# Attention b: the row maxima moved into the query tiles by one transpose, one copy and two small transfers

## The chip, the cores and the metric

The kernel runs on one core of a Trainium2 chip. The metric is the device time of one execution in microseconds (us). The core has five engines, each of which takes its own instructions in order: PE (TensorE, matrix multiplies and transposes; its weight loads are shown as PEld), DVE (VectorE), ACT (ScalarE), POOL (GpSimd) and SP (SyncE, which here only starts DMA transfers). Engines wait for each other by semaphores.

## What is computed

Four layers are added to a residual x of 2 x 512 x 512 numbers: attention a, a mixture of experts, attention b, and the same mixture of experts again. The change is in attention b, cut here to what matters (B = 2, T = 512, 32 query heads, 8 key heads, 16 numbers each):

```python
x = x + _L0_attn_b_ref(_layernorm(x, axis=-1), Wq, Wk, Wv, Wo)
...
att = jnp.einsum('bhgqd,bhkd->bhgqk', qg, k) / math.sqrt(D_HEAD)
att = jnp.where(causal[None, None, None], att, -jnp.inf)
probs = jax.nn.softmax(att, axis=-1)
ctx = jnp.einsum('bhgqk,bhkd->bhgqd', probs, v)
```

The softmax needs the largest score of every query. The kernel finds it in a first pass over the scores and subtracts it in a second one.

## The kernel before

Attention a comes first (to about 720 us in the trace). Then comes a short stretch of experts and projections, and then the stage of attention b, which this change is in: it begins with the first score at 792.6 us and the last product of the second pass begins at 1025 us. What follows is the end of attention b for the second batch entry and the last experts.

**Pairs and steps.** The heads of attention b are worked on in 32 pairs (`pairs`). A pair takes 3 steps (`STEPS`), and there are 104 steps. PE's order is written out by hand (`manual_schedule` for PE); the order on the other engines is made by the framework's scheduler. A step emits, in this order: now and then the loading of query rows (`queries_halved`, `queries_in`); in one step of three, `maxima_in` for a pair; a third of `probabilities` for a pair; a third of `maxima` for a later pair; sometimes four calls of `weighted_b`; and a piece of side work (projections of the second batch entry, later the output projection and the experts).

**First pass**, `maxima` (lines 765 to 797), pair p in steps 3p to 3p+2. PE multiplies queries by keys into PSUM tiles `sc` (line 781), and DVE adds the causal mask and takes the maxima into a small tile `top` (line 785): a query on each of 128 partitions, 4 query tiles, 2 heads. After the last part POOL splits each maximum into a rounded part and a rest (lines 793 and 794). They go into a tile `mm` of 4 x 66 columns, of which only columns 0, 1 and 64, 65 are ever filled; two such tiles exist, and both are set to zero once (line 609).

**Into rows**, `maxima_in` (lines 799 to 807), in step 3p+4. The second pass needs the maxima in rows 64 and 65 of the query tile `qs`, one row for the rounded parts and one for the rests, 2 heads x 512 queries each. The keys hold -1 in those rows, so that the product of keys and queries comes out with the maximum subtracted. PE transposes the four 66-column parts of `mm` into one PSUM tile `tpm` (line 804), and ACT copies two rows of it for each head into `qs` (line 807).

**Second pass**, `probabilities` (lines 812 to 845), pair p in steps 3p+8 to 3p+10 (`LEAD` is 8). PE multiplies keys by queries, the maximum included, into PSUM tiles `st` (line 828); ACT takes the exponential (line 834); POOL clears the part above the diagonal (line 837). `weighted_b` then multiplies by the values on PE (line 854). It runs for two pairs together.

**Shared buffers.** `sc`, `st` and `tpm` use one ring of five PSUM banks (`ps_x`), in the order in which they are emitted. A tile waits until the one five places before it has been read: `sc` by DVE, `st` and `tpm` by ACT. There are five query tiles `qs`. Pair p uses the tile of pair p-5, and its load (line 761, on SP) and the clearing of its rows 64 and 65 by POOL (line 763, needed because the first pass must not see old maxima) are emitted in step 3p-4. Both wait for the last `st` of pair p-5.

The lines which place these calls in a step are:

```python
            if at == 0 and 2 <= p < len(pairs):
                queries_in(p)
            p, at = divmod(step - 4, STEPS)
            if at == 0 and 0 <= p < len(pairs):
                maxima_in(p)
            if LEAD <= step:
                next(ps)
            if step < total:
                next(ms)
```

Of the kernel before, what the change touches and what calls it, by code (L numbers as in the profile page):

```python
# [11 lines left out]
F32 = mybir.dt.float32  # L12
I32 = mybir.dt.int32
F32R = mybir.dt.float32r
AF = mybir.ActivationFunctionType
ALU = mybir.AluOpType
# [3 lines left out]
P = 128  # L20
B, S, DM = 2, 512, 512
NT = S // P
# [18 lines left out]
def kernel(  # L41
# [21 lines left out]
    nc = tc.nc  # L63
# [3 lines left out]
    small = ctx.enter_context(tc.tile_pool(name="small", bufs=4))  # L67


    x = {}  # L70
# [7 lines left out]
    ident = const.tile([P, P], F32, tag="ident", name="ident")  # L78
# [201 lines left out]
    with ExitStack() as actx:  # L280
# [226 lines left out]
        def chain(*stages):  # L507
            for stage in stages:
                yield from stage
# [13 lines left out]
        for n in range(len(units) + 4):  # L523
            turn = []

            def at(lag):
                if 0 <= n - lag < len(units):
                    g, b, h = units[n - lag]
                    return (g, b, h, f"{g}_{b}_{h}")

            if at(3):
                g, b, h, nm = at(3)
# [4 lines left out]
            if at(0):  # L537
                g, b, h, nm = at(0)
# [8 lines left out]
            if at(4):  # L547
                g, b, h, nm = at(4)
                turn.append(output(wo[g], h, g * A_G + h, b, *ats.pop((g, b, h)), nm))
            if at(2):  # L550
                g, b, h, nm = at(2)
# [22 lines left out]
    w2 = ctx.enter_context(tc.tile_pool(name="w2", bufs=1))  # L574
# [11 lines left out]
    for sp in range(4):  # L586
        for par in range(2):
            at = sp * STRIP + par * B_HD
# [9 lines left out]
    HALF, HM = P // 2, P // 2 + 2  # L598
    NQ = 5
    qs = [w2.tile([P, 2, S], F32, tag=f"qs{n}", name=f"qs_{n}") for n in range(NQ)]  # L600
    ks = [w2.tile([P, 4, S], F32, tag=f"ks{n}", name=f"ks_{n}") for n in range(2)]

    mmp = [w2.tile([P, NT, HM], F32R, tag=f"mm{n}", name=f"mm_{n}") for n in range(2)]

    vpads = [
        w2.tile([P, NT, 2, 4, STRIP], F32, tag=f"vpad{n}", name=f"vpad_{n}") for n in range(B)
    ]
    for pad in (*ks, *qs, *vpads, *(mm.bitcast(F32) for mm in mmp)):
        nc.gpsimd.memset(pad, 0.0)
    for pad in ks:  # L610
        nc.gpsimd.memset(pad[HALF:HM], -1.0)
# [10 lines left out]
    dram = ctx.enter_context(tc.tile_pool(name="dram", bufs=2, space=bass.MemoryType.DRAM))  # L622
# [99 lines left out]
    STEPS, LEAD = 3, 8  # L722
    mms, nums, oNs, pTs = {}, {}, {}, {}
# [6 lines left out]
    def spread(hl, nm, order):  # L730
# [5 lines left out]
            )  # L736
        return to.rearrange("n (d h) s -> (n d) h s", h=B_NKV)

    kparts, qparts = {}, {}

    def keys_in(b, kh):

        if kh == 0:
            kparts[b] = spread(khls[b], f"k_{b}", (slice(0, 4, 2), slice(1, 4, 2)))
        nc.sync.dma_start(ks[kh][:HALF], kparts[b][:, ts(kh, 4), :])

    def queries_halved(p):

        b, kh, g, _ = pairs[p]
        hl = hlp.tile([P, 2, S], F32R, tag="hl", name=f"hl_{p}")  # L750
        src = qTs[b][:, kh * 2 + g // 2, :]
        nc.scalar.copy(hl[:, 0, :], src)
        nc.gpsimd.tensor_tensor(hl[:, 1, :], src, hl[:, 0, :].bitcast(F32), ALU.subtract)
        to = spread(hl, f"q_{p}", (slice(0, 2), slice(2, 4)))
        for n in range(4):
            qparts[p + n] = to

    def queries_in(p):
        _, _, g, pr = pairs[p]
        q = qs[p % NQ]  # L760
        nc.sync.dma_start(q[:HALF], qparts.pop(p)[:, ts((g % 2) * 2 + pr, 2), :])
        if p >= NQ:
            nc.gpsimd.memset(q[HALF:HM], 0.0)

    def maxima():

        for p, (b, kh, g, pr) in enumerate(pairs):
            q, k = qs[p % NQ].bitcast(F32R), ks[kh].bitcast(F32R)
            top = small.tile([P, NT, 2], F32, tag="top", name=f"top_{p}")
            for tiles in ((0, 1), (3,), (2,)):  # L770
                sc = [
                    ps_x.tile([P, S], F32, tag="x", name=f"sc_b_{p}_{tiles[0]}_{h}")
                    for h in range(2)
                ]
                parts, at = [], 0
                for i in tiles:
                    n = (i + 1) * P
                    parts += [(i, n, h, sc[h][:, at : at + n]) for h in range(2)]
                    at += n
                for i, n, h, part in parts:  # L780
                    nc.tensor.matmul(  # L781
                        part, q[:, h, ts(i, P)], k[:, pr * 2 + h, :n], start=True, stop=True
                    )
                for i, n, h, part in parts:
                    nc.vector.tensor_tensor_reduce(  # L785
                        part, part, tri[:, S - n :], 1.0, -3e38, ALU.add, ALU.max,
                        top[:, i, h : h + 1],
                    )
                if tiles == (2,):
                    mm = mms[p] = mmp[p % len(mmp)]  # L790
                    for h in range(2):
                        at = (1 - h) * HALF
                        nc.gpsimd.tensor_copy(mm[:, :, at], top[:, :, h])
                        nc.gpsimd.tensor_tensor(
                            mm[:, :, at + 1], top[:, :, h], mm[:, :, at].bitcast(F32), ALU.subtract
                        )
                yield

    def maxima_in(p):

        mm = mms.pop(p).bitcast(F32)
        tp = ps_x.tile([P, S], F32, tag="x", name=f"tpm_{p}")
        for t in range(NT):
            nc.tensor.transpose(tp[:HM, ts(t, P)], mm[:, t, :], ident)
        for h in range(2):
            at = (1 - h) * HALF
            nc.scalar.copy(qs[p % NQ][HALF:HM, h, :].bitcast(F32R), tp[at : at + 2, :])


    due = []  # L810
# [92 lines left out]
    def output_b(b, cs):  # L903

        while not all((b, c) in ready for c in cs):
            yield MM
        for i in range(NT):
            po = place("bank", [P, DM], f"po_{b}_{i}_{cs[0]}")
            for c in cs:
                nc.tensor.matmul(  # L910
                    po, oNs[b, c][:, ts(i, P)], wo2[:, c, :], start=(c == cs[0]), stop=(c == cs[-1])
                )
                if c == cs[-1]:
                    nc.vector.tensor_tensor(x[b, i], x[b, i], po, ALU.add)
                yield MM

    def run(*stages):
        stages = list(stages)
        while stages:
            stages = [st for st in stages if next(st, stages) is not stages]  # L920
# [18 lines left out]
    for p in range(2):  # L939
        queries_in(p)  # L940
    parts(later, 14)

    ms, ps = maxima(), probabilities()
    total = len(pairs) * STEPS
    half = total // 2
# [3 lines left out]
    for step in range(total + LEAD):  # L949
        with tc.manual_schedule(engines={mybir.EngineType.PE}):  # L950
            if step == LEAD:
                pace = 0.95
            if step == half - 4:
                run(side)
                keys_in(1, 0)
                queries_halved(len(pairs) // 2)
                side = output_b(0, (0, 1))
                pace, left = 0.37, 0.0
            if step == half + LEAD:
                keys_in(1, 1)  # L960
            if step == half + LEAD + 10:
                side = chain(side, output_b(0, (2, 3)), experts(0, "f2", True))
                pace, left = 0.95, 0.0
            if step == total - 6:
                side = chain(output_b(1, (0, 1)), side)
                pace, left = 1.4, 0.0
            quotients[:] = [q for q in quotients if next(q, None) is not None]
            p, at = divmod(step + 4, STEPS)
            if at == 0 and p % 4 == 3 and p + 1 < len(pairs) and p + 1 != len(pairs) // 2:
                queries_halved(p + 1)  # L970
            if at == 0 and 2 <= p < len(pairs):
                queries_in(p)
            p, at = divmod(step - 4, STEPS)
            if at == 0 and 0 <= p < len(pairs):
                maxima_in(p)
            if LEAD <= step:
# [4 lines that stand above are left out]
            if len(due) > 3 and due[3][0] <= step:  # L981
                for _ in range(4):
                    weighted_b(*due.pop(0)[1])
            left += pace
            while left > 0:
                got = next(side, None)
                if got is None:
                    left = 0.0
                else:
                    left -= got  # L990
# [99 lines left out]
```

## Time and profile before

| what | value |
|---|---|
| median of 3 runs | 1092.24 us (1091.74 to 1095.13) |
| the profiled execution's own time | 1095.07 us |
| its span, first to last instruction | 1093.4 us |
| PE busy | 1046.9 us, 96% of the span |
| DVE busy | 859.0 us, 79% |
| ACT busy | 627.2 us, 57% |
| POOL busy | 598.5 us, 55% |
| TensorE clock granted, mean | 0.992 of full speed |

The profiled execution is one of its own and lies 2.8 us above the median of the runs; 1.7 us of its time are outside the span. A busy share is an average over the whole span. What a change is worth must be read from the stage that it is in. In rows of the profile, a time in ns is the mean of one instruction, and what stands after the second bar is how long the engine was idle just before, with the instruction whose end it waited for. DMA-issuing instructions are not counted as busy.

### The profile page before, as it was taken

How to read it: one execution, taken by the hardware profiler on the slowest of the kernel's cores; microseconds unless marked ns; L12 is line 12 of the kernel's file. 1: busy time of each engine (PE TensorE's matmuls, PEld its weight loads, DVE VectorE, ACT ScalarE, POOL GpSimd, SP SyncE). 2: the span in 40 equal slices, each digit the busy share in tenths (PEclk: the TensorE clock that was granted, in tenths of full speed). 3: DMA queues.
4: the chain of work that ended last, by engine and by line, in shares of the span. 5: the costliest groups of instructions: out<-in, count | busy, mean ns of one | idle time of the engine just before them, and what ended most of it. 6: DMA issues, size and time to landing. Idle time of an engine off the chain costs nothing.

```text
span 1093.4 us, 16248 instructions
## 1 busy us (share of the span) xinstructions
PE 1046.9 (96%) x4940; PEld 707.0 (65%) x4940; DVE 859.0 (79%) x2175; ACT 627.2 (57%) x1475; POOL 598.5 (55%) x916
## 2 busy tenths in 40 slices
PE   5799999999999999999999999999999999999988
PEld 3477767777777677777777777556467655565534
DVE  6889899999999999999999999574386667766142
ACT  3666666567666566566666665513166567685410
POOL 2466666677576666666666666262245566554200
PEclk9999999999999999999999999999999999999999
DMA  7301011012110010010021000042342235211011
GB/s 294 116 1 39 1 39 39 1 39 78 39 40 25 16 39 20 20 39 12 28 75 42 1 1 1 1 155 75 87 161 83 57 122 149 88 49 35 28 38 39
DMA packets 23271, 60.47 MB, mean 55 GB/s; under 512 B 4369, under 2 KB 5329, under 8 KB 20369
## 3 DMA queue, kind: packets, MB, share of 16 engines
q1 hardware_dynamic: 23184, 59.44, 16.4%
q8 instruction: 40, 0.66, 0.2%
q14 instruction: 47, 0.38, 0.1%
HBM read 45.53 MB, written 12.85 MB: 53 GB/s over the span
## 4 chain that ended last, share of the span: by engine, by line
PE 80%; DVE 9%; ACT 4%; issue 2%; POOL 2%; DMA 2%; SPq 0%; ACTq 0%; POOLq 0%; DVEq 0%
PE sc L412 11%; PE av L445 11%; PE tp L440 6%; PE ph_f L207 5%; PE ps_q L365 5%; PE ps_o L457 5%; PE ps_o L458 5%; PE ps_q L366 4%; PE st_b L828 4%; PE py_f L266 3%; PE sc_b L781 3%; PE num_b L854 3%; PE po L910 3%; PE pq_b L701 2%; DVE r_q L372 1%
## 5 line engine op out<-in xcount | busy, mean ns | idle before, releaser
L429 POOL TENSOR_SCALAR p<-p,rden 128x128 f32<-128x128 f32 (+3 forms) x256 | 152.4, 607 | 227.0 <-DVE rden L427 167.1
L420 ACT ACTIVATE p<-sc,nmx 128x128 f32<-128x128 f32 (+3 forms) x256 | 135.8, 530 | 110.3 <-DVE nmx L415 108.7
L412 PE MATMUL sc<-kT,qT 128*128 128x128 f32 (+3 forms) x512 | 180.5, 435 | 1.7 <-ACT p L420 1.3
L372 DVE SCALAR_TENSOR_TENSOR r_q<-ps_q,s_q,r_q 128x512 f32<-128x512 f32 x192 | 143.8, 749 | 20.6 <-PE ps_q L366 16.3
L467 DVE SCALAR_TENSOR_TENSOR acc<-ps_o,s_o,acc 128x512 f32<-128x512 f32 x186 | 137.5, 744 | 19.9 <-PE ps_o L458 17.7
L785 DVE CUSTOM_DVE_ANT_0 sc_b<-sc_b,tri 128x128 f32<-128x128 f32 (+3 forms) x256 | 119.8, 517 | 42.2 <-PE sc_b L781 27.8
L445 PE MATMUL av<-pT,v 128*128 128x512 f32 (+3 forms) x512 | 148.5, 433 | 0.0
L445 PEld LDWEIGHTS av<-pT,v 128*128 128x128 f32 x512 | 96.7, 189 | 64.2 <-issue 36.2
L415 DVE CUSTOM_DVE_ANT_0 sc<-sc,tri 128x128 f32<-128x128 f32 (+3 forms) x256 | 125.9, 492 | 11.2 <-PE sc L412 10.3
L441 ACT COPY pT<-tp 128x128 f32<-128x128 f32 (+3 forms) x256 | 108.2, 423 | 46.0 <-PE tp L440 45.6
L365 PE MATMUL ps_q<-xh,w_q 128*128 128x512 f32 x256 | 121.1, 473 | 3.0 <-ACT r_v L370 1.4
L440 PE MATMUL tp<-ident,p 128*128 128x128 f32 x640 | 114.2, 274 | 3.2 <-POOL p L429 1.6
L412 PEld LDWEIGHTS sc<-kT,qT 128*128 128x128 f32 x512 | 94.9, 189 | 27.6 <-ACT p L420 6.9
L457 PE MATMUL ps_o<-ah,w_o 128*128 128x512 f32 x256 | 110.4, 431 | 1.8 <-DVE acc L467 1.2
L366 PE MATMUL ps_q<-xl,w_q 128*128 128x512 f32 x256 | 101.6, 397 | 0.0
L458 PE MATMUL ps_o<-al,w_o 128*128 128x512 f32 x256 | 101.2, 395 | 0.0
L834 ACT ACTIVATE pT_b<-st_b 128x384 f32<-128x384 f32 (+1 forms) x192 | 89.8, 529 | 17.8 <-PE st_b L828 16.7
L440 PEld LDWEIGHTS tp<-ident,p 128*128 128x128 f32 x640 | 78.5, 140 | 31.6 <-issue 8.7
L837 POOL TENSOR_SCALAR_AFFINE_SELECT pT_b<-pT_b 128x128 f32<-128x128 f32 (+1 forms) x192 | 63.4, 339 | 63.6 <-ACT pT_b L834 59.6
L387 POOL TENSOR_TENSOR r_q<-r_q,tab 128x512 f32<-128x512 f32 x64 | 82.2, 1284 | 9.1 <-DVE rs_q L384 9.1
L465 POOL TENSOR_TENSOR acc<-acc,part 128x512 f32<-128x512 f32 x62 | 80.0, 1290 | 11.5 <-ACT part L464 11.5
L388 POOL TENSOR_TENSOR qT<-r_q,rs_q 128x512 f32<-128x512 f32 x64 | 82.6, 1291 | 5.0
(179 smaller groups left out, 2062.9 us busy)
## 6 DMA issues: line engine op xcount, KB each, us to landing
codes_q<-in_q_codes_dram SPq DMA_DIRECT2D x8, 1024.0 KB
codes_o<-in_o_codes_dram SPq DMA_DIRECT2D x8, 1024.0 KB
spread_q<-hl SPq DMA_DIRECT2D x16, 512.0 KB
qs<-spread_q SPq DMA_DIRECT2D x32, 256.0 KB
x_a<-in_x_dram SPq DMA_DIRECT2D x8, 256.0 KB
codes_k<-in_k_codes_dram SPq DMA_DIRECT2D x2, 1024.0 KB
codes_v<-in_v_codes_dram SPq DMA_DIRECT2D x2, 1024.0 KB
x_r<-in_x_dram SPq DMA_DIRECT2D x8, 256.0 KB
```

The costliest lines, as they stand in the source:

```text
L365: nc.tensor.matmul(ps, w[:, c, ts(h, A_HD)], xh[b][:, c, :], start=True, stop=False)
L366: nc.tensor.matmul(ps, w[:, c, ts(h, A_HD)], xl[b][:, c, :], start=False, stop=True)
L372: nc.vector.scalar_tensor_tensor(r, ps, s, r, ALU.mult, ALU.add)
L412: nc.tensor.matmul(sc[:, :n], qT[:, ts(i, P)], kT[:, :n], start=True, stop=True)
L415: nc.vector.tensor_tensor_reduce(sc[:, :n], sc[:, :n], tri[:, S - n :], -(A_HD**-0.5), 3e38, ALU.add, ALU.min, nmx,)
L420: nc.scalar.activation(pr, sc[:, :n], AF.Exp, bias=nmx, scale=-1.0, accum_out=den[:, i % 2 : i % 2 + 1],)
L429: nc.gpsimd.tensor_scalar(prs[j], prs[j], rden[:, j % 2 : j % 2 + 1], 1.0, ALU.mult, ALU.mult)
L440: nc.tensor.transpose(tp[:, j, :], prs[i][:, ts(j, P)], ident)
L445: nc.tensor.matmul(av[:, j * P :], v[:, j, :], pT[:, j, j * P :], start=(j == 0), stop=(j == NT - 1))
L457: nc.tensor.matmul(ps, w[:, h, ts(n, P)], ah, start=True, stop=False)
L458: nc.tensor.matmul(ps, w[:, h, ts(n, P)], al, start=False, stop=True)
L467: nc.vector.scalar_tensor_tensor(to, ps, s, to, ALU.mult, ALU.add)
```

## The change

The maxima of a pair become 16 columns: 8 rounded parts and 8 rests, each ordered by head and query tile. POOL writes them with two instructions in place of four, into a tile of 128 x 16 that comes from a pool of three (`tops`) and needs no zeros. PE makes one transpose of 16 columns, in step 3p+5 in place of 3p+4. ACT copies the 16 x 128 result into a tile `mx` and then issues two DMA transfers on its own queue: 8 rows of `mx` into row 64 of the query tile and 8 into row 65, 4 KB each. The rows are cleared no longer by POOL but by a transfer on SP's queue, of 8 KB of zeros from DRAM, that is issued right behind the load of the query rows. The zeros are stored to DRAM once, before the stage, from two rows of a key tile.

```diff
-    mmp = [w2.tile([P, NT, HM], F32R, tag=f"mm{n}", name=f"mm_{n}") for n in range(2)]
+    tops = ctx.enter_context(tc.tile_pool(name="tops", bufs=3))
...
-    for pad in (*ks, *qs, *vpads, *(mm.bitcast(F32) for mm in mmp)):
+    for pad in (*ks, *qs, *vpads):
...
+    none = dram.tile([2, 2, S], F32, tag="none", name="none", bufs=1)
+    nc.sync.dma_start(none, ks[0][HM : HM + 2, :2, :])
...
         if p >= NQ:
-            nc.gpsimd.memset(q[HALF:HM], 0.0)
+            nc.sync.dma_start(q[HALF:HM], none)
...
-            top = small.tile([P, NT, 2], F32, tag="top", name=f"top_{p}")
+            top = small.tile([P, 2 * NT], F32, tag="top", name=f"top_{p}")
...
-                    mm = mms[p] = mmp[p % len(mmp)]
-                    for h in range(2):
-                        at = (1 - h) * HALF
-                        nc.gpsimd.tensor_copy(mm[:, :, at], top[:, :, h])
-                        nc.gpsimd.tensor_tensor(
-                            mm[:, :, at + 1], top[:, :, h], mm[:, :, at].bitcast(F32), ALU.subtract
-                        )
+                    mm = mms[p] = tops.tile([P, 2, 2 * NT], F32R, tag="mm", name=f"mm_{p}")
+                    nc.gpsimd.tensor_copy(mm[:, 0, :], top)
+                    nc.gpsimd.tensor_tensor(
+                        mm[:, 1, :], top, mm[:, 0, :].bitcast(F32), ALU.subtract
+                    )
...
-        for t in range(NT):
-            nc.tensor.transpose(tp[:HM, ts(t, P)], mm[:, t, :], ident)
-        for h in range(2):
-            at = (1 - h) * HALF
-            nc.scalar.copy(qs[p % NQ][HALF:HM, h, :].bitcast(F32R), tp[at : at + 2, :])
+        rows = 4 * NT
+        nc.tensor.transpose(tp[:rows, :P], mm.rearrange("p x n -> p (x n)"), ident)
+        mx = tops.tile([rows, P], F32, tag="mx", name=f"mx_{p}")
+        nc.scalar.copy(mx.bitcast(F32R), tp[:rows, :P])
+        q = qs[p % NQ]
+        for n in range(2):
+            nc.scalar.dma_start(
+                q[HALF + n : HALF + n + 1].rearrange("p h (t n) -> p (h t) n", n=P),
+                mx[ts(n, rows // 2), :],
+            )
...
-            p, at = divmod(step - 4, STEPS)
+            p, at = divmod(step - 5, STEPS)
```

As the changed program is built, ACT's queue holds for a pair: the copy into `mx`, the exponential of the first `st` of the pair before, the two DMA issues, the exponential of the second `st`. On PE the transpose stands just ahead of these two `st`.

More of the change, by code (lines that the diff above doesn't have):

```diff
@@ L786, in maxima @@
                         part, part, tri[:, S - n :], 1.0, -3e38, ALU.add, ALU.max,
-                        top[:, i, h : h + 1],
+                        top[:, h * NT + i : h * NT + i + 1],
                     )
                 if tiles == (2,):
-                    mm = mms[p] = mmp[p % len(mmp)]
-                    for h in range(2):
-                        at = (1 - h) * HALF
-                        nc.gpsimd.tensor_copy(mm[:, :, at], top[:, :, h])
-                        nc.gpsimd.tensor_tensor(
-                            mm[:, :, at + 1], top[:, :, h], mm[:, :, at].bitcast(F32), ALU.subtract
-                        )
+                    mm = mms[p] = tops.tile([P, 2, 2 * NT], F32R, tag="mm", name=f"mm_{p}")
[3 more added lines that the diff above has]
+                    )
                 yield
```

## Prediction

> **What bounds the kernel now.** I read the page's engine shares and chain first.
>
> ```profile
> span 1093.4 us, 16248 instructions
> ...
> PE 1046.9 (96%) x4940; PEld 707.0 (65%) x4940; DVE 859.0 (79%) x2175; ACT 627.2 (57%) x1475; POOL 598.5 (55%) x916
> ...
> PE 80%; DVE 9%; ACT 4%; issue 2%; POOL 2%; DMA 2%; SPq 0%; ACTq 0%; POOLq 0%; DVEq 0%
> ```
>
> The chain that ended last runs through PE for 80% of the span, so PE is the engine to watch. Next comes the busy time of the stage alone, from the first transposes of maxima to the last.
>
> ```profile
> 797.00:1016.00 219.00, 208.26 (x1284) 132.96 (x1286) 150.61 (x592) 147.43 (x300) 122.92 (x353) 0.98 0.28 86
> ```
>
> The columns are window, length, busy PE, PEld, DVE, ACT, POOL, clock, DMA share, GB/s. PE is busy for 208 of 219 us, DVE 151, ACT 147, POOL 123. PE paces the stage, and nobody else is full. The groups of that window which the change touches:
>
> ```profile
> L834 ACT ACTIVATE pT_b<-st_b 128x512 f32<-128x512 f32 (+1 forms) x182 | 85.2, 530 | 15.8 <-PE st_b L828 14.8
> L828 PE MATMUL st_b<-qs,ks 128*128 128x512 f32 (+1 forms) x242 | 76.2, 408 | 1.7 <-ACT qs L807 1.1 <-DVE top L785 0.2
> ...
> L807 ACT CAST qs<-tpm 2x512 fp32r<-2x512 f32 x64 | 36.8, 575 | 24.7 <-PE tpm L804 24.0
> ...
> L763 POOL MEMSET qs<- 2x1024 f32 x27 | 25.5, 945 | 21.7 <-PE st_b L828 21.4
> ...
> L804 PE MATMUL tpm<-ident,mm 128*66 128x128 f32 x128 | 20.5, 284 | 4.1 <-POOL mm L794 3.7
> ...
> L804 PEld LDWEIGHTS tpm<-ident,mm 128*66 128x66 f32 x128 | 13.9, 117 | 14.0 <-POOL mm L794 8.1 <-issue 4.8 <-POOL pT_b L837 0.7
> ```
>
> The 284 ns of a transpose are its latency. What it takes of PE is the distance between starts, seen in the timeline of PE over one pair (start, length, instructions):
>
> ```profile
> 945.87 0.60 PE L804 MATMUL tpm<-ident,mm 128*66 128x128 f32 x4
> ...
> 947.94 1.03 PE L828 MATMUL st_b<-qs,ks 128*128 128x512 f32 x2
> 948.80 0.51 PE L781 MATMUL sc_b<-ks,qs 128*128 128x384 f32 x2
> 949.15 1.02 PE L910 MATMUL po<-wo,oN_b 128*128 128x512 f32 x2
> 949.61 0.92 PE L828 MATMUL st_b<-qs,ks 128*128 128x384 f32 x2
> 950.37 0.62 PE L781 MATMUL sc_b<-ks,qs 128*128 128x128 f32 x4
> ```
>
> Four transposes end 0.60 us after the first began and the last takes 0.27, so they start (0.60 - 0.27) / 3 = 0.11 us apart (0.109 as the median of all 32 pairs).
>
> **PE: a gain.** A pair loses three of four transposes: 3 x 0.109 x 32 = 10.5 us of PE's stream. The one that stays has 16 columns in place of 66; I take no gain for that. Moved by a step (1.7 us or more), it no longer waits for POOL's `mm`, which in ten of 32 pairs ended just before it: PE's 3.7 us of idle time go (with PEld's 8.1 as the upper end, since most of those lie under a running matmul). `st` waiting for the bank that ACT's two copies hold cost PE 1.1 + 0.2 us (the 0.2 ahead of `sc`); the bank is now free after 0.3 us of copy in place of 1.16, so 1.3 us go. Together 15.5 us.
>
> **ACT: about even, but at another place.** Removed are 2 x 0.575 = 1.15 us a pair. Added is one copy of 16 x 128 (nearest row: the 128 x 128 cast of `khl`, 0.27 us) and two DMA issues. ACT issues none before; SP's issues of 4 to 16 rows take 0.51 to 0.69 us (`dens_b`, `oN_b`), its shortest of the stage 0.32. I take 0.55 each: 1.1 a pair. These stand between the exponentials of the first and the second `st`. ACT in that pair:
>
> ```profile
> 946.51 1.16 ACT L807 CAST qs<-tpm 2x512 fp32r<-2x512 f32 x2 [1.00 <-PE tpm L804]
> ...
> 948.77 1.09 ACT L834 ACTIVATE pT_b<-st_b 128x512 f32<-128x512 f32 x2 [0.20 <-PE st_b L828]
> ```
>
> The second exponential ends at 949.86. In the new order of banks it must be read before the `sc` that starts at 950.37: 0.51 us of slack. Read so for every pair, 14 pairs have 1.9 to 3.2 us (`num_b`, 2.3 us of PE, lies between), and the 15 others, such as this one, have a median of 0.51 and a mean of 0.34. If ACT's sequencer works through the issues while the first exponential (0.6 us) runs, the second is 1.1 - 0.6 = 0.5 late; over the 15 pairs what exceeds each slack sums to 3 us. If it stands until the first has ended, the second is 1.1 late: 11.4 us. The trace shows ACT's semaphore instructions starting inside a running copy (938.63, in the copy that begins at 938.40), so I take 3 us and keep 11.4 as an end.
>
> The Trainium skill ("DMA: Bandwidth & Descriptors", section "Issuing engines are not separate DMA queues") says that the time a sequencer spends on starting a DMA is usually small beside the DMA; by that this term would be 0. The rows here speak against it: 0.53 us of issue in 1.93 from issue to use. Its section "Rules for kernel authors" asks for small transfers to be joined; by that rule two transfers of 4 KB are the wrong form.
>
> **The transfers: hidden, with a margin.** No row shows a 4 KB move on ACT's queue. The nearest small load into SBUF, 32 KB:
>
> ```profile
> 1032.28 0.53 SPq L887 DMA_DIRECT2D sums_b<-dens_b  x1
> ```
>
> ```profile
> 1034.21 0.55 DVE L890 RECIPROCAL sums_b<-sums_b 128x64 f32<-128x64 f32 x1 [0.60 <-DMA sums_b<-dens_b]
> ```
>
> From issue to use 1.93 us. From the first `st` of the pair before, the chain is: 0.75 to the start of its exponential, by which the copy is over; two issues, 1.1; and 1.93 - 0.53 = 1.4 after the last issue. That is 3.3 us, or 3.9 if ACT stands. It must end before this pair's own first `st`, one pair later: the starts of first `st` lie 4.96 to 9.2 us apart (mean 7.05), every second one near 5.5. The margin is 1.1 us or more, so I take nothing. Upper end: 256 KB loads take 3.6 us in the chain of waits (`qs<-spread_q`), and if the small ones end behind such a load, 2.2 us are added.
>
> `st` now also waits for two transfers; a semaphore instruction of PE's sequencer takes 51 ns: 64 x 0.051 = 3.3 us at most, none where PE is behind. I take 2.
>
> **POOL, DVE and SP: nothing.** POOL loses 27 memsets (25.5 us), the 21.7 us that it stands before them, and half of its small instructions. It is busy for 123 of 219 us; PE waited for it only at `tpm`, counted above, and DVE for some 7 us (waits by `sc_b` L785), with DVE far from full. SP gains 27 issues of some 0.5 us, each directly behind a query load with the same wait; queued behind it are the next query loads and the `dens_b` chain. The query loads are issued 11 to 13 us before their first `sc` (pairs 5 to 7), so 0.5 us more hides; the cover is thinnest at pair 16 (4.7 us), which has the zeros ahead of its load. If it fails there, 0.5 to 2 us once. The store of the zeros and the two memsets saved (2 x 0.59) lie at 720 to 745 us, before the first use.
>
> **The sum.** 15.5 - 3 - 2 = 10.5, rounded to 10 us. On the profiled execution that is 1095.07 - 10 = 1085. The median of the runs shown is 2.8 lower, and I predict for it: 1092.2 - 10 = 1082 us. About 0.3% (3.3 us) is what a measurement of this kernel can tell from no change.
>
> **The rivals.**
>
> *ACT stands while it issues* (0.20). The second exponential is then 1.1 us late and PE waits for its bank in every second pair: 15.5 - 11.4 - 2 = 2 us gained, 1090 (1089 to 1095). For it: PEld already waits 10.6 us for exponentials ahead of `st`. Against it: the sequencer that runs ahead. DVE or ACT taking over as the bound would look the same.
>
> *All of the waits go* (0.10). The LDWEIGHTS waits were real PE time: 10.5 + 11.8 (POOL) and no loss gives 22 us: 1070 (1065 to 1076).
>
> *The maxima arrive late* (0.18; slower). The transfers share the DMA engines with the query spreads and loads (DMA share 0.52 from 890 to 920 us) and `st` of every second pair stands for them. It turns the sum when some 16 pairs lose more than (10 + 3.3) / 16 = 0.8 us beyond the margin of 1.1 to 1.6, so when issue to use grows from 1.93 to about 4.1. At 4.5 to 5 us it costs 16 x 1.3 = 21 us or so: 1092 + 11 = 1103 (1096 to 1110). For it: this wait is new, and the step given up was 2 us of lead. Against it: 0.28 as the stage's mean DMA share.
>
> The forecast itself (1077 to 1088) gets 0.52. Faster: 0.52 + 0.10 = 0.62; within 0.3%: 0.20; slower: 0.18. The range 1070 to 1099 leaves out the lower half of the second rival (0.05) and two thirds of the third (0.12).
>
> **What would show it.** Right: `tpm` is 32 transposes of some 0.3 us latency without idle time for POOL; the copy about 0.27 us; the stage from 797 shorter by about 10 us; little PE or PEld time waiting for DMA ahead of `st`. Wrong: PEld `st_b` or `sc_b` idle for ACT grows by over 8 us (first rival); a line "PE st_b <- DMA qs<-mx" of over 10 us (third); or ACT's issues taking 1 us and more, which I have priced at 0.55.

## The result, and the profile after

The changed kernel takes 1097.24 us (median of 20 runs, 1094.11 to 1101.83), the kernel before 1092.8 (20 runs, 1090.93 to 1095.13). The ratio is 1.0044, 95% interval 1.0035 to 1.0054: slower by some 4.8 us, where 10 us less (1082) were predicted. One point of ratio below (0.01) is 10.9 us.

The page of the changed kernel has the same shape as before, with less PE work (1039.7 us for 1046.9) in a longer span:

```profile
span 1095.4 us, 16046 instructions
...
PE 1039.7 (95%) x4844; PEld 697.2 (64%) x4844; DVE 860.2 (79%) x2175; ACT 600.1 (55%) x1443; POOL 562.1 (51%) x823
```

The chain of waits is of no use here: it could be followed back over 14% of the span only. The window of the stage answers better (window, length, busy PE, PEld, DVE, ACT, POOL, clock, DMA share, GB/s):

```profile
797.00:1016.00 219.00, 200.00 (x1169) 122.94 (x1168) 151.84 (x596) 117.49 (x262) 86.10 (x258) 0.96 0.30 91
```

PE was idle for 10.7 of these 219 us before, and is idle for 19.0 now; the granted clock fell from 0.98 to 0.96. The groups of the window that answer to those of before:

```profile
L840 ACT ACTIVATE pT_b<-st_b 128x512 f32<-128x512 f32 (+1 forms) x178 | 86.5, 529 | 55.5 <-PE st_b L834 34.3 <-DMA qs<-mx 9.4 <-PE sc_b L784 5.3
L834 PE MATMUL st_b<-qs,ks 128*128 128x512 f32 (+1 forms) x238 | 75.2, 408 | 14.7 <-DVE top L788 11.0 <-DMA qs<-mx 3.2
...
L834 PEld LDWEIGHTS st_b<-qs,ks 128*128 128x128 f32 x239 | 39.7, 198 | 44.9 <-DVE top L788 23.6 <-issue 10.4 <-DVE mv_b L164 2.8
L805 PE MATMUL tpm<-ident,mm 128*16 128x128 f32 x31 | 8.8, 283 | 1.2 <-POOL pT_b L843 0.7 <-DVE top L788 0.3 <-DVE x_r L270 0.2
L807 ACT CAST mx<-tpm 16x128 fp32r<-16x128 f32 x31 | 7.8, 252 | 19.3 <-PE tpm L805 19.1
```

The transposes are down to 31 in the window and wait no longer for POOL's `mm`, and the copy takes 0.252 us. The new thing is in `st`: PE stands 11.0 us and its weight load 23.6 us until DVE has finished a `top`, that is, has read a tile `sc`. In the kernel before, the same waits were short (us in total, times, longest):

```profile
PE st_b L828 <- DVE top L785: 0.2, 1, 0.2
PEld st_b L828 <- DVE top L785: 1.1, 4, 0.5
```

`st` takes nothing from DVE. What it waits for there is a PSUM bank that a tile `sc` still holds.

The transfers themselves show little: PE waits for `qs<-mx` 3.2 us, in two places. One is the first `st` of the stage (start, length, idle time before):

```profile
801.21 1.90 ACTq L810 DMA_DIRECT2D qs<-mx  x2
...
806.10 1.19 PE L834 MATMUL st_b<-qs,ks 128*128 128x512 f32 x2 [2.64 <-DMA qs<-mx]
```

**The banks.** The programs as built show which bank each tile got. The text on the kernel before said that a tile takes the bank of the tile five places earlier. That was wrong, and the prediction rests on it: the framework's scheduler (the "planner" of the expectations) hands out the five banks anew in each program and not in turn. By what rule it does so, the programs don't show. Of 411 tiles `sc`, `st` and `tpm`, 277 had the bank of the tile five places earlier in the kernel before and 10 one of three places or fewer; in the changed kernel it is 141 and 63. (The expectations of the strict runs count 281 and 145 at five places; the built programs give 277 and 141.) Most of the near ones are of one kind: 45 tiles `st` of the changed kernel have a bank that an `sc` took three places before or fewer, against 6 in the kernel before. In 26 cases `st` of tile 3 has the bank that an `sc` took only two places before.

### The profile page after: what moved, and what is told of

The parts are those of the page before. It is cut to its first block, busy times and chain, and to the rows that moved or that the text cites. A ratio compares the mean times of both kernels' runs of the same rounds, so it can differ in the third digit from the quotient of the medians.

```text
span 1095.4 us, 16046 instructions
## 1 busy us (share of the span) xinstructions
PE 1039.7 (95%) x4844; PEld 697.2 (64%) x4844; DVE 860.2 (79%) x2175; ACT 600.1 (55%) x1443; POOL 562.1 (51%) x823
## 5 line engine op out<-in xcount | busy, mean ns | idle before, releaser
L840 ACT ACTIVATE pT_b<-st_b 128x384 f32<-128x384 f32 (+1 forms) x192 | 93.1, 528 | 59.0 <-PE st_b L834 36.8
L834 PE MATMUL st_b<-qs,ks 128*128 128x256 f32 (+3 forms) x256 | 80.8, 409 | 14.7 <-DVE top L788 11.0
```

## The experiments

All times are medians of 4 to 12 runs; each ratio is against the kernel before, run on the same chip, and the ratios are what can be compared between rows. Four kernels leave the maxima out of the exponent (after_no_transfers, after_idle_transfer, after_act_busy, idle_banks_of_after) and two take the maxima of half of the keys (after_half_reduce, before_half_reduce); these six are yardsticks and not versions to use.

| run | us | ratio, 95% | tiles 5 places / up to 3 |
|---|---|---|---|
| strict_before | 1098.42 | 1.0054 (1.0034 to 1.0073) | 411 / 0 |
| strict_after | 1096.37 | 1.0044 (1.0028 to 1.0059) | 411 / 0 |
| after_two_memsets | 1096.64 | 1.0039 (1.0023 to 1.0054) | 141 / 63 |
| before_shift | 1092.47 | 1.0005 (0.9991 to 1.0019) | 242 / 42 |
| after_four_transposes | 1104.41 | 1.0110 (1.0087 to 1.0134) | 166 / 53 |
| after_no_transfers | 1077.39 | 0.9868 (0.9848 to 0.9888) | 230 / 40 |
| after_half_reduce | 1087.33 | 0.9959 (0.9946 to 0.9971) | 156 / 66 |
| before_half_reduce | 1086.14 | 0.9944 (0.9926 to 0.9963) | 211 / 40 |
| after_idle_transfer | 1082.77 | 0.9900 (0.9881 to 0.9919) | 204 / 37 |
| after_act_busy | 1079.73 | 0.9870 (0.9846 to 0.9893) | 220 / 43 |
| after_sp_issue | 1087.99 | 0.9941 (0.9922 to 0.9960) | 245 / 28 |
| after_pool_issue | 1082.87 | 0.9897 (0.9876 to 0.9918) | 233 / 37 |
| after_banks_of_pool | 1089.98 | 0.9980 (0.9971 to 0.9988) | 198 / 38 |
| pool_banks_of_after | 1099.70 | 1.0065 (1.0049 to 1.0080) | 133 / 76 |
| idle_banks_of_after | 1100.83 | 1.0081 (1.0067 to 1.0095) | 126 / 80 |
| pool_two_memsets | 1082.06 | 0.9910 (0.9897 to 0.9923) | 233 / 37 |
| pool_own_banks | 1083.70 | 0.9897 (0.9881 to 0.9913) | 233 / 37 |
| after_rows_by_pool | 1105.61 | 1.0104 (1.0087 to 1.0121) | 146 / 60 |

**1. Strict rotation, the shift, and two memsets.** In the strict kernels every tile of the stage asks for the next of five banks, and the whole loop is one hand-written order for PE. The last four pieces of work ahead of the loop move to the banks of the side work (`BESIDE`).

```diff
-    for step in range(total + LEAD):
-        with tc.manual_schedule(engines={mybir.EngineType.PE}):
+    with tc.manual_schedule(engines={mybir.EngineType.PE}):
+        for step in range(total + LEAD):
...
-                    ps_x.tile([P, S], F32, tag="x", name=f"sc_b_{p}_{tiles[0]}_{h}")
+                    x_bank(f"sc_b_{p}_{tiles[0]}_{h}")
...
+    def x_bank(name):
+        turn.append(name)
+        return ps_x.tile([P, S], F32, tag=f"x{len(turn) % 5}", name=name)
...
-    parts(later, 14)
+    parts(later, 10)
+    banks[:] = BESIDE
+    parts(later, 4)
```

> The kernel before with one edit: each of the tiles sc_b, tpm and st_b of the stage takes the next of the five banks in turn, in the order in which the loop writes them, and PE runs the whole loop in the written order. In the kernel before, 281 of 411 of these tiles already take the bank of the tile five places earlier and 73 take one that is less than five places back. Both theories expect little: 1091 to 1094 us, within 0.2% of before. It is the yardstick for the next run.

> The changed kernel with the same edit. There only 145 of 411 tiles take the bank of the tile five places earlier, 146 a nearer one, 28 of them the bank of two tiles before, and PE and its weight load stand 34.6 us before st_b for DVE's reduce in the stretch from 797 to 1016 us. Theory A (the banks that the planner hands out in the changed kernel make PE stand for DVE): those waits go, and with them the loss; 1082 to 1088 us, that is 5 to 10 us under the strict kernel before. Rival B (ACT's two issues a pair, at 0.627 us each, and the transfers are the cost): 1095 to 1098 us, as the changed kernel. Between them, 1089 to 1094, would mean that the banks are a part only.

The loss stayed: 1.0044, and 1096.4 lies in rival B's range. Theory A, as I had put it, fell. In the strict changed kernel PE stands before `sc` instead. The window and PE's `sc` of strict_before:

```profile
797.00:1016.00 219.00, 204.81 (x1246) 132.35 (x1245) 149.51 (x589) 143.21 (x291) 120.36 (x344) 0.95 0.29 86
```

```profile
L786 PE MATMUL sc_b<-ks,qs 128*128 128x512 f32 (+1 forms) x244 | 63.5, 359 | 6.8 <-DVE top L790 3.3 <-ACT pT_b L839 2.7 <-DVE mv_b L164 0.2
```

And of strict_after:

```profile
797.00:1016.00 219.00, 197.57 (x1169) 120.90 (x1168) 150.63 (x593) 118.31 (x263) 87.20 (x258) 0.97 0.30 90
```

```profile
L789 PE MATMUL sc_b<-ks,qs 128*128 128x128 f32 (+1 forms) x248 | 67.2, 357 | 14.2 <-DVE top L793 8.0 <-ACT pT_b L845 5.6
L789 PEld LDWEIGHTS sc_b<-ks,qs 128*128 128x128 f32 x247 | 40.8, 195 | 32.4 <-DVE top L793 18.8 <-ACT pT_b L845 9.5 <-issue 0.8
```

The yardstick was not neutral either (strict_before lost 0.0054), so an even distance is no cure, and the distance by itself not the measure. These two runs have the ring that the prediction assumed, and with it the change brings 2.0 us (1098.4 to 1096.4; the intervals overlap) and not 10: PE's idle time in the window grows from 14.2 to 21.4 us. They do not separate the rotation from the fixed order of PE.

```diff
-            p, at = divmod(step - 4, STEPS)
+            p, at = divmod(step - 5, STEPS)
```

> The kernel before, with the maxima moved to their rows one step later (step - 5 for step - 4) and nothing else. It keeps the four transposes, the two copies and no transfer. Theory A: the shift by itself makes the planner hand out other banks (242 of 411 at five places, 85 nearer, 42 of them two or three places), so a loss of 1 to 5 us, 1093 to 1098. Rival B: 1091 to 1093, as before.

The shift alone costs nothing that can be measured, as rival B had it, though its banks are less regular than before's.

```diff
-    for pad in (*ks, *qs, *vpads):
+    mmp = [w2.tile([P, NT, HM], F32R, tag=f"mm{n}", name=f"mm_{n}") for n in range(2)]
+    for pad in (*ks, *qs, *vpads, *(mm.bitcast(F32) for mm in mmp)):
```

> The changed kernel with the two clearings of tiles mm put back (1.13 us on POOL ahead of those of ks), though nothing uses those tiles now; everything else is instruction for instruction the changed kernel. Theory (without them POOL's two long memsets, 2.0 us each, fall beside two of DVE's four tensor_scalars xn_f, 2.105 us each in place of about 0.6, and the stage begins 1.2 to 1.5 us later): 1095.5 to 1096.3, about 1.2 us under the changed kernel. Rival (that start is hidden): no change, 1097.2.

The collision is real in the trace (shown at the end) and moved the first score back from 794.1 to 792.6 us, but the time by 0.6 us, within the intervals.

**2. Is it PE's work, the transfers, or DVE's reduces?**

```diff
-        nc.tensor.transpose(tp[:rows, :P], mm.rearrange("p x n -> p (x n)"), ident)
+        for t in range(NT):
+            nc.tensor.transpose(tp[:rows, ts(t, P)], mm.rearrange("p x n -> p (x n)"), ident)
```

> The changed kernel, but TensorE does four transposes a pair again, all of the same 16 columns into four parts of tpm, of which only the first is read: the 96 transposes come back at 0.109 us, 10.5 us of PE, and nothing else. Theory C (PE waits in this stage for the others whatever it does, so what it saves is stood out before the next bank: from before to after its work falls 8.7 us and its idle time rises 8.3): 0 to 3 us slower than the changed kernel, 1097 to 1100. Rival (PE's work sets the stage, and the loss is in fixed stalls, late maxima at pairs 0 and 19 with the half clock behind them): 8 to 11 us slower, 1105 to 1108.

1104.4, 7.2 us over the changed kernel and just under the rival's range: PE's work seems to count, so that the gain of the transposes was there and something larger ate it. It is no clean price, since the banks moved too: 335 of 411 tiles follow the same tile on their bank as in the changed kernel.

```diff
-        for n in range(2):
-            nc.scalar.dma_start(
...
```

> The changed kernel without the two transfers a pair that move the maxima: ACT issues nothing, nothing lands late, and the rows stay cleared (the maxima are left out of the exponent). Theory T (late maxima at the first pair, PE idle from 803.2 to 806.1, then 10.2 us at half clock, another 2.6 us at pair 19, and 1.3 us of ACT a pair cost it): 6 to 12 us faster than the changed kernel, 1085 to 1091. Theory C (PE waits for DVE's reduces and for the banks in any case): 0 to 3 us faster, 1094 to 1097.

1077.4, under both ranges: without the transfers the change would bring 14.4 us, and with them it loses 4.8. The 19 us between are more than theory T could name. The banks are another set here (230 and 40). The window:

```profile
797.00:1016.00 219.00, 211.83 (x1287) 131.31 (x1286) 150.38 (x599) 125.32 (x283) 92.31 (x274) 0.98 0.30 90
```

```diff
-                        part, part, tri[:, S - n :], 1.0, -3e38, ALU.add, ALU.max,
+                        part[:, : n // 2], part[:, : n // 2], tri[:, S - n : S - n // 2], 1.0, -3e38, ALU.add, ALU.max,
```

> The changed kernel with DVE's eight reduces a pair over half of their columns (the maxima are of half of the keys), so that DVE is done sooner with each bank. Theory C: PE's 10.2 and 8.8 us of idle time in the two halves of the stage shrink to half or less, 8 to 12 us faster than the changed kernel, 1085 to 1089. Theory T: the late transfers stay, 0 to 4 us faster, 1093 to 1097.

> The kernel before with the same halved reduces. Theory C: PE is then the bound, so the saved transposes show as the difference between this run and the one above: here 1088 to 1092, 3 us or more above the changed kernel with halved reduces, up to the 8.7 us of work. Theory T: 1 to 4 us under the kernel before and under the changed one with halved reduces, as without halving: 1088 to 1092 here against 1093 to 1097 there.

Sooner reads help both kernels (by 0.0085 and 0.0056), but the changed one does not pass the other. Neither theory foresaw both: the changed kernel lies in C's range, but C wanted it 3 us or more below the other, and it came out 1.2 us above; T wanted 1093 to 1097 for it.

**3. What about the transfers costs 19 us?**

```diff
+        aside = tops.tile([rows, P], F32, tag="aside", name=f"aside_{p}", bufs=1)
         for n in range(2):
-            nc.scalar.dma_start(
-                q[HALF + n : HALF + n + 1].rearrange("p h (t n) -> p (h t) n", n=P),
-                mx[ts(n, rows // 2), :],
-            )
+            nc.scalar.dma_start(aside[ts(n, rows // 2), :], mx[ts(n, rows // 2), :])
```

> The changed kernel, but ACT's two transfers a pair go to a small tile of 16 rows that nothing reads (the maxima are left out of the exponent). ACT issues as many transfers, of as many bytes, and nobody waits for them to land. Without any transfer the kernel took 1077.4 us. Theory I (ACT's issues, 1.28 us a pair, delay the exponentials and so the banks): 1090 to 1098. Theory L (PE waits for what lands, at the first pairs above all): 1077 to 1082.

```diff
-            nc.scalar.dma_start(
...
+            junk = tops.tile([rows, NT, P], F32, tag="junk", name=f"junk_{p}_{n}", bufs=1)
+            nc.scalar.copy(junk, mx.unsqueeze(1).to_broadcast([rows, NT, P]))
```

> The changed kernel without its transfers (the maxima are left out of the exponent), but with two copies on ACT in the place of the two issues: 16 rows x 512 elements, which by the copies of the kernel before (0.58 us) take 1.16 us a pair against 1.28 of the issues. Theory I: 1088 to 1096, most of the 19 us between this and the changed kernel are back. Theory L: 1077 to 1082.

Theory I, as a cause of the 19 us, fell: issues with traffic but no waiter cost 0.0032, 3.5 us, beside no transfers (the intervals just overlap), and 38.6 us of copies on ACT (64 x 603 ns) cost nothing that can be measured (0.9870 and 0.9868). These are bounds and no prices: the banks differ between the three, and the copies lie one behind each of the two exponentials where the issues lie both between them.

```diff
-            nc.scalar.dma_start(
+            nc.sync.dma_start(
```

> The changed kernel with the two transfers issued by SP. ACT is free of 41 us, and the rows land through SP's queue. Theory I: 1078 to 1086. Theory L: 1092 to 1102, since SP's queue puts them behind its other transfers.

```diff
-            nc.scalar.dma_start(
+            nc.gpsimd.dma_start(
```

> The changed kernel with the two transfers issued by POOL, which is free for half of the stage. No run here shows what an issue costs on POOL. Theory I: ACT is free of 41 us, 1078 to 1090, the upper end if POOL's issues delay the affine selections. Theory L: 1092 to 1102.

Theory L fell with these: `st` waits for the same rows (PE stands 5.5 us for them with POOL's issues, 3.2 us in the changed kernel), and the kernel computes the same, yet it takes 1082.9 with POOL's issues, in theory I's range, and 1088.0 with SP's, between the two ranges. Both beat the kernel before. The order of PE's instructions is not the difference: the changed kernel's differs from that of after_idle_transfer by 17 short moves in 3820 instructions. The banks differ throughout.

**4. The exchange of banks.** Each tile of the stage is given, by name, the bank that it has in another kernel (with the `BESIDE` lines of the strict kernels, but without their one hand-written order).

```diff
-                    ps_x.tile([P, S], F32, tag="x", name=f"sc_b_{p}_{tiles[0]}_{h}")
+                    x_bank(f"sc_b_{p}_{tiles[0]}_{h}")
...
+        bank = BANKS.split()[int(p)][n]
+        return ps_x.tile([P, S], F32, tag=f"x{bank}", name=name)
```

> The changed kernel, with ACT's issues and all of its waits, but every tile sc_b, tpm and st_b takes the bank that the planner gave it in the kernel with POOL's issues (given by name; 198 of 411 then lie five places apart, 38 two or three, against 141 and 63). Theory B (the hand-out of banks is the loss): 1081 to 1088. Theory W (a wait for a transfer of ACT's queue is the loss): 1094 to 1099, as the changed kernel.

> The kernel with POOL's issues (1082.9 us), but every tile of the three kinds takes the bank that it has in the changed kernel (133 five places apart, 76 two or three). Theory B: 1091 to 1099. Theory W: 1082 to 1086.

> The kernel whose transfers nobody awaits (1082.8 us; the maxima are left out of the exponent), with the banks of the changed kernel (126 five places apart, 78 two or three). Theory B: 1091 to 1099. Theory W: 1082 to 1086.

> The control of the exchange: the kernel with POOL's issues, with its own banks named by hand in the same manner as in the three runs with exchanged banks. If the banks are the cause: 1082 to 1084, as without naming (1082.9). If the naming is the cause: 1090 to 1100.

The changed kernel's banks cost POOL's kernel 0.0168 (18 us) and the kernel that awaits no transfer 0.0181 (20 us), a little more than theory B's range; naming a kernel's own banks costs nothing (0.9897 both times, tried on POOL's kernel). PE's order moves slightly with the exchange, by 41 to 55 short moves in 3820 instructions. `st` of after_pool_issue, with its own banks:

```profile
L834 PE MATMUL st_b<-qs,ks 128*128 128x256 f32 (+3 forms) x256 | 78.0, 402 | 6.6 <-DMA qs<-mx 5.5 <-ACT mx L807 0.4 <-DVE top L788 0.4
```

And with the banks of the changed kernel, where PE stands for DVE as it does there:

```profile
L840 PE MATMUL st_b<-qs,ks 128*128 128x128 f32 (+2 forms) x240 | 76.7, 413 | 11.9 <-DVE top L794 6.5 <-DMA qs<-mx 4.9
```

The window, and `st` in it, of after_idle_transfer with its own banks:

```profile
797.00:1016.00 219.00, 208.02 (x1235) 128.29 (x1234) 150.29 (x598) 123.71 (x277) 89.76 (x268) 0.97 0.31 93
```

```profile
L832 PE MATMUL st_b<-qs,ks 128*128 128x512 f32 (+1 forms) x252 | 79.1, 409 | 1.4 <-DVE top L788 1.0 <-ACT mx L807 0.3
...
L832 PEld LDWEIGHTS st_b<-qs,ks 128*128 128x128 f32 x252 | 41.7, 196 | 28.1 <-issue 16.1 <-ACT pT_b L838 4.8 <-DVE top L788 3.6
```

And with the banks of the changed kernel:

```profile
797.00:1016.00 219.00, 199.48 (x1157) 121.90 (x1157) 150.28 (x593) 114.64 (x258) 84.99 (x252) 0.95 0.31 93
```

```profile
L838 PE MATMUL st_b<-qs,ks 128*128 128x128 f32 (+3 forms) x232 | 75.7, 418 | 13.8 <-ACT pT_b L844 7.4 <-DVE top L794 5.0 <-ACT mx L813 0.7
...
L838 PEld LDWEIGHTS st_b<-qs,ks 128*128 128x128 f32 x232 | 40.0, 201 | 45.2 <-ACT pT_b L844 15.5 <-DVE top L794 14.8 <-issue 9.7
```

PE's idle time before `st` goes from 1.4 to 13.8 us, its weight load's from 28.1 to 45.2, and PE's share of the window falls to that of the changed kernel (199.5 and 200.0 us), although nobody waits for a transfer.

The other way, POOL's banks in the changed kernel, the exchange gave 0.0064 only, 7.0 us: 1090.0, between the theories' ranges, but faster than the kernel before (0.9980). PE hardly stands for DVE before `st` there:

```profile
L840 PE MATMUL st_b<-qs,ks 128*128 128x512 f32 (+2 forms) x242 | 77.4, 413 | 6.2 <-DMA qs<-mx 3.4 <-ACT pT_b L846 2.4
```

The other 0.0083 (9 us) up to POOL's kernel stay open. In another kernel a set of banks no longer fits the order that it came from (of the 233 tiles at five places 198 are left), and whether that mismatch or the queue of the issues makes the rest was not separated. A mismatch may also be part of the 18 and 20 us (141 and 63 become 133 and 76, 126 and 80). The 7.0 us were gained in spite of one, so at least these are due to the changed kernel's own banks. The banks of the kernel before were not tried in the changed one.

**5. The best version, and the clearing alone.** after_pool_issue beats both kernels (0.9897). With the two memsets put back:

> The kernel with POOL's issues and the two clearings of the unused tiles mm put back, so that POOL's long memsets lie beside one of DVE's tensor_scalars xn_f and not beside two; the banks are the same. By the changed kernel's pair of runs (1097.2 and 1096.6): 0 to 1.3 us faster than 1082.9, 1081.5 to 1083. Both theories say so; it is a version to set against the two kernels.

No further gain can be seen (0.9910, intervals overlap).

```diff
-            nc.sync.dma_start(q[HALF:HM], none)
+            nc.gpsimd.memset(q[HALF:HM], 0.0)
```

> The changed kernel with the rows cleared by POOL's memset again, ahead of the transfers, and without tile none and its transfers. The banks stay nearly those of the changed kernel (146 five places apart against 141, 60 two or three against 63). If the clearing by a transfer costs nothing, as predicted: 1096 to 1099. If the clearing transfers on SP's queue are part of the loss: 1088 to 1094.

Outside both ranges, on the far side: POOL's clearing costs 0.0060, 6.6 us, with nearly the same banks (379 of 411 tiles follow the same tile on their bank), so here the clearing by a transfer was a gain. Where POOL clears, it stands in its own queue for `st` of the pair whose tile it clears, and `mm` and the affine selections behind it must wait too. How that reaches PE was not followed up; the granted clock of the window falls from 0.96 to 0.93. POOL's memset:

```profile
L763 POOL MEMSET qs<- 2x1024 f32 x27 | 25.8, 956 | 38.8 <-PE st_b L831 35.3 <-issue 3.1
```

## Why the prediction was wrong

- **The step that failed** is "In the new order of banks it must be read before the `sc`", and behind it the whole sum of 15.5 us: the banks were taken as a fixed ring and every other wait as unchanged, so that waits could only vanish with what held a bank. The banks are handed out anew for each program. In the set that came out PE stands 11.0 us ahead of `st` for DVE, where the sum had no term ("POOL, DVE and SP: nothing"). That the set costs time is shown by the exchange: 18 and 20 us in two other kernels, and 7.0 us in the changed kernel itself, enough to turn its loss into a small gain. The other 8 us from that run (1090) to the forecast (1082) stay open. Why this set came out was not tried.
- **A true ring would not have saved the sum.** Where both kernels have one (strict_before, strict_after, with PE's order fixed as well) the change brings 2.0 us, within the intervals, and PE stands longer before `sc` for DVE and ACT. So the step from PE work saved to time saved fails there too.
- **None of the three signs of being wrong came.** The weight load's idle time for exponentials ahead of `st` did not grow but fell (10.6 to 2.4 us), PE stood 3.2 us for `qs<-mx`, and an issue took 0.627 us in the median. The sign was a wait for DVE, which was not on the list.
- **PE's 10.5 us of transposes**: right in kind. Put back, they cost 7.2 us, with somewhat other banks.
- **POOL's `mm` and the copies' banks (3.7 and 1.3 us)**: these waits went, as the rows show. In before_shift POOL's wait alone goes, by a later step, and nothing is gained; its banks differ as well.
- The 15.5 us gained on PE stand beside 14.4 us measured without the transfers, but the 14.4 hold the clearing and another set of banks as well, so the agreement proves no single term and may be chance.
- **ACT, 3 us for a later exponential**: an issue took 0.627 us where I had 0.55. The first did run beside the exponential, and the second exponential came 0.8 us late and not 0.5 (the trace has 12 such waits of ACT, 10.2 us in all). What that costs PE was not isolated: some 3.5 us by after_idle_transfer at its own banks, but the 9 us between after_banks_of_pool and after_pool_issue, which share a set of banks, may hold some of it. The pair at 863 us (start, length, instruction, idle time before it):

```profile
863.48 0.26 ACT L807 CAST mx<-tpm 16x128 fp32r<-16x128 f32 x1 [0.73 <-PE tpm L805]
863.70 0.60 ACT L840 ACTIVATE pT_b<-st_b 128x512 f32<-128x512 f32 x1
...
863.79 1.29 ACTq L810 DMA_DIRECT2D qs<-mx  x2
...
865.13 0.60 ACT L840 ACTIVATE pT_b<-st_b 128x512 f32<-128x512 f32 x1 [0.83 <-DMA qs<-mx]
```

- **Transfers hidden**: mostly right. By after_idle_transfer issues and traffic cost some 3.5 us (with its own banks), and PE awaited the rows for 3.2 us, at two pairs. From the start of the second issue to the last packet they took 1.38 us in 13 of 32 pairs and up to 5.26 (pair 19). The rival "the maxima arrive late" had the sign and nearly the time, but by luck: its mechanism decides at two pairs and not at sixteen.
- **Clearing, "nothing"**: wrong. In the changed kernel POOL's clearing costs 6.6 us; I had looked for PE waiting on POOL, not for what stands behind the memset.
- **The two memsets saved, "nothing"**: in the time, yes; in the trace the stage began later by 1.4 us.
- **No step** spoke of the clock: see below.

## What to carry to other kernels

Where a framework assigns PSUM banks, an edit that only changes when a tile is due can change the assignment, so list bank and predecessor of each tile in both built programs before pricing a change, and if a loss appears, exchange the two assignments before blaming the edit. Do it both ways, since a set may also cost time because it does not fit the other program. An instruction that waits at the head of a busy engine's queue delays what stands behind it, so look there before you put it at nothing. Try a transfer's issue on each engine that could make it: here the same two transfers gave 1097, 1088 and 1083 us from ACT, SP and POOL, with another set of banks each time, so that the figures price the whole program and not the issue.

## What the runs showed of the hardware

**Half clock after a slack stretch.** The first `st` came late, and PE was busy for 0.82 of 3.41 us. Then the granted clock (the column before the DMA share) was 0.50 for 10.2 us:

```profile
802.48:805.89 3.41, 0.82 (x4) 0.19 (x2) 3.41 (x15) 1.04 (x2) 0.39 (x2) 1.00 0.65 239
805.89:809.30 3.41, 3.12 (x8) 2.22 (x9) 2.62 (x11) 3.37 (x6) 0.36 (x2) 0.50 0.00 0
809.30:812.71 3.41, 2.96 (x12) 2.27 (x12) 3.41 (x15) 1.98 (x5) 3.34 (x8) 0.50 0.16 35
812.71:816.13 3.42, 3.42 (x15) 3.05 (x13) 1.85 (x8) 1.24 (x3) 0.95 (x3) 0.50 0.71 264
```

Before, the slack stretch had 2.01 us of work and the half clock lasted 3.41:

```profile
805.57:808.98 3.41, 2.01 (x14) 1.56 (x13) 2.82 (x14) 3.35 (x5) 2.04 (x6) 1.00 0.27 100
808.98:812.40 3.42, 3.42 (x12) 2.72 (x12) 2.53 (x7) 3.36 (x8) 2.60 (x5) 0.50 0.83 286
```

So a stall of PE is paid once more: by an estimate from these rows, 6.8 us more at half clock are up to 3.4 us of PE. The Trainium skill ("TensorE: Matmul & The Clock Gate", section "Part 1: The HAM clock gate") says that the clock follows how busy PE has been in windows of 3413 ns and halves after at least one idle window. The 3.41 us agree; the rows show that the window need not be idle: one with PE 59% busy, by the trace's modelled matmuls, was enough.

**DVE beside POOL's memsets.** Without the two memsets of `mm`, both memsets of `ks` lie beside DVE's four tensor_scalars (start, length). Before:

```profile
732.61 3.94 DVE L173 TENSOR_SCALAR xn_f<-x_r,mv_f,rstd_f 128x512 f32<-128x512 f32 x4
733.11 1.13 POOL L609 MEMSET mm<- 128x264 f32 x2
734.30 3.99 POOL L611 MEMSET ks<- 2x2048 f32 x2
```

After:

```profile
732.86 5.58 DVE L173 TENSOR_SCALAR xn_f<-x_r,mv_f,rstd_f 128x512 f32<-128x512 f32 x4
733.48 3.99 POOL L611 MEMSET ks<- 2x2048 f32 x2
```

Beside the 2 us memsets one tensor_scalar before and two after took 2.105 us; the other five took 0.61 to 0.84.

**Issues.** The same transfer takes 0.627 us to issue on ACT, 0.646 on SP and 0.541 on POOL (medians of 64).
